# A three-part decoder layer on one core: feed-forward bias in row groups, reciprocal parts on another engine, input loads on another queue, and a new planned order

## The chip, the core and the metric

The kernel runs on one core of a Trainium2 chip. The core has a matrix engine (TensorE, PE in the profile, with its weight loads as PEld), three engines for elementwise work (VectorE or DVE, ScalarE or ACT, GpSimd or POOL) and SyncE (SP), which issues DMAs. All of them run at the same time, each through its own queue of instructions in order. The metric is the device time of one execution in microseconds (us).

## The reference

Eight sequences of 256 tokens with 512 features pass a self-attention with rotary positions, a cross-attention to a second input of the same shape, and a feed-forward part; behind each stands a layer norm of the sum with its input. The change touches what lies around the feed-forward part:

```python
def activation_quant(x):
    scale = 127.0 / jnp.clip(jnp.max(jnp.abs(x), axis=-1, keepdims=True), EPS, None)
    return jnp.clip(jnp.round(x * scale), -128.0, 127.0) / scale
def weight_quant(w):
    scale = 1.0 / jnp.clip(jnp.mean(jnp.abs(w)), EPS, None)
    return jnp.clip(jnp.round(w * scale), -1.0, 1.0) / scale
def bitlinear(x, w, b):
    return jnp.einsum('bsd,fd->bsf', activation_quant(x), weight_quant(w)) + b
h = bitlinear(x, w1, b1)                 # 512 -> 2048
h = jax.nn.gelu(h, approximate=False)
h = layernorm(h, gamma, beta)            # over 2048
return bitlinear(h, w2, b2)              # 2048 -> 512
```

## The kernel before, in words

The 2048 tokens are 16 tiles (tt) of 128. The residual lies in SBUF for the whole run as `acc`, 16 tiles of 128x512.

The first part, up to about 942 us, is the self-attention, with an order written out by hand (`SCHED`). The change does not touch it.

Everything after it is one planned stage. Each function (`kv`, `q`, `x`, `ffn_tables`, `ffn`) only records steps with `S(...)`: a step has one or more choices of engine with a cost in us, the tiles that it reads, writes and makes, and a function that issues its instructions. The planner at the end of `decoder_kernel` then plays the stage in its own clock: it takes the ready step with the lowest priority number that finds its engine and its buffers free, notes where it runs, and at last issues all steps in that order, engine by engine. Priorities come from `PLAN["base"]` (one number per unit of work), `PLAN["off"]` (small offsets per step) and the step's distance from its unit's end. `PLAN["lim"]` and `PLAN["cap"]` limit buffers, `PLAN["eng"]` fixes the engine of each step that has a choice, and `PLAN["T"]` says when a step of the other activation table may be taken; exponentials have table E and gelus table G. "DVE+" and "POOL" steps share a port in the planner's model, "POOL-" steps hold it shortly. So a changed cost or a changed PLAN moves instructions of the whole stage, not of one place.

The units of the stage:

- `kv(bp)`: keys and values of the cross-attention, four times 512 tokens, eight products of 12 matmuls each (kvp), written to DRAM.
- `q(b)`: the first layer norm and the transposes of two token tiles (tp), and for each second b the query product (qp).
- `x(b)`, per sequence: scores (sc, L880), exponentials (pt, L884), clamps with the mask (L888), sums (den, L911) and values (av, L895); the reciprocal of the sums spread by a small matmul (rp, L930) and multiplied into u (L933); then per token tile the split cT (L950 to L952), the output product (xo), two norms, and the quantised input of the feed-forward part. `stats` (L753, L754) or `astats` on ScalarE (L757 to L761) take mean and variance; `rstd` (L764, L765) and `scale1` (L967 to L969) on GpSimd make the reciprocal deviations; `absmax` (L985 to L987) the scale of the quantisation; L1004 and L1008 the rounding into xq; L1006 adds b2 to `acc`.
- `inverse` in `x` (L993 to L1001, GpSimd): the bias b1 is added by the matmul that also multiplies x with the weights. The matmul's sum is later scaled by a1s, so b1 has to come in divided by that scale. `inverse` puts the reciprocal of the scale, split in three bf16 parts, as columns 0, 32, 64 (three times the first part), 33, 65 (twice the second) and 66 of a block of 128 columns beside the 512 quantised values in xq, and zeros in the rest.
- The xq of 128x640 is transposed by a DMA into xT (L1010) and written to DRAM as xqs (L1011).
- `ffn_tables`: loads the quantised weights (fw0, fw1), gamma, beta, and b1 broadcast to 96 rows (b1r), split in bf16 parts in rows 0 to 31, 32 to 63 and 64 to 95 of b1s (L1034, L1036); csp and csum correct an offset of the second product.
- `ffn(tt)`, per token tile: load xqs as xx (`load`, issued at L714 by SyncE); two groups of ten matmuls (up): per 512 columns four with xx (L1070) and one of 96 rows for the bias (L1071); gelu with accumulated sum (L1075); mean (L1080), square (L1084) and `spread` (L1089 to L1091) for the norm over 2048; the norm itself for the half hi on VectorE (L1095, L1108) and for the half lo on ScalarE, VectorE and GpSimd (L1103, L1105, L1107); the maxima (L1111), `scale` (L1116 to L1118), L1121 on GpSimd; rounding into hq (L1124 ScalarE or L1125 VectorE); a DMA transpose into hT (L1153, for the last tile by TensorE, L1145); 17 matmuls (dn, L1131, L1133); y (L1155), its norm (L753, L754, L764, L765, L768, then L1160 VectorE or L1161 ScalarE) and the store of y (L1162).

Of the kernel before, what the change touches and what calls it, by code (L numbers as in the profile page):

```python
# [37 lines left out]
PLAN = {  # L38
    "base": {"c": [-3437], "wq": [-222], "wo": [2567], "kv": [774, 529, 640, 738], "q": [186, 220, 195, 464, 52, 506, 393, 405], "x": [-2946, -2928,
        -3094, -2933, -2926, -2955, -2930, -3031], "w": [2222], "f": [2732, 2741, 2722, 2769, 2648, 2719, 2728, 2753, 2749, 2721, 2720, 2716, 2739,  # L40
        2743, 2683, 2745]},
    "off": {"c": {0: 7, 1: -21, 3: 15, 4: 25, 5: 7, 7: -17, 8: -3, 9: 5}, "f": {0: -13, 1: 1, 2: -8, 3: 5, 5: -6, 6: 15, 9: -10, 10: -3, 11: 21, 12:
        16, 13: 5, 14: -20, 15: 12, 16: 20, 17: 7, 19: 7, 20: 2, 21: 3, 22: 30, 23: 5, 24: 3, 25: 27, 26: 5, 27: 11, 28: 10, 29: -8, 30: 2}, "kv": {1:
        3, 2: -9, 6: -23, 7: 10, 8: -3, 9: 5, 10: 3, 11: 9, 12: 3, 13: -22, 14: -6, 17: 11, 18: -3, 19: 24, 21: 17, 22: 3, 24: -11, 25: 5, 26: -6, 27:
        18, 28: -8, 29: -9}, "q": {0: 15, 5: 1, 6: -14, 7: 3, 8: 2, 9: 23, 12: 1, 13: -9, 14: -6, 15: -18, 16: 6, 17: -3, 18: 7, 19: -5, 21: -1}, "w":
        {0: -12, 1: -10, 2: 9, 3: 19, 5: 15, 6: 9, 7: 8, 9: -8, 12: -27, 14: -21, 16: -1, 17: -27, 18: 1, 19: -10}, "wo": {0: 6, 2: 4, 3: -27, 5: 1},
        "wq": {0: -16, 2: 6, 3: -21}, "x": {0: -3, 2: -16, 3: 10, 5: 13, 6: -2, 7: -18, 9: -8, 10: 6, 11: -9, 12: 4, 13: 12, 15: -3, 16: 10, 17: -3,
        19: -12, 20: -3, 23: -3, 24: 20, 25: 3, 26: -3, 28: -4, 29: -2, 30: -12, 31: -23, 32: -4, 33: 2, 34: 2, 36: 1, 38: 1, 39: -3, 41: -3, 42: 11,
        44: 6, 45: 8, 46: -4, 47: -1, 48: -7, 51: -1, 52: -13, 53: -17, 54: 18, 55: -4, 56: -20, 57: -5, 58: -1, 59: 8, 60: 14, 61: -14, 63: -7, 64:
        -8, 65: 10, 68: -5, 69: -11, 70: 10, 72: -11, 73: -3, 76: 3}},  # L50
    "lim": {"wqraw": 1, "kvp": 3, "kvs": 4, "cr": 1, "woraw": 1, "x1T": 1, "qst": 3, "tp": 1, "qp": 2, "kx": 2, "vx": 1, "u": 1, "rr": 2, "rs": 1,
        "den": 2, "pt": 4, "sc": 2, "av": 2, "rp": 2, "cT": 1, "d": 2, "xq": 2, "xT": 3, "xo": 2, "b1r": 1, "xx": 1, "h": 4, "hq": 3, "hT": 3, "y": 3,
        "up": 2, "dn": 1},
    "cap": {"p8": 6, "p4": 6, "p2": 9},
    "T": 1158, "hx": 1, "dve": [15], "sum": [],
    "eng": "0--1110100-0-010-0101-1-1-0--0-010-0-1-00-0-10-010-0101-1-1--010--1-00-11-000--0-010-010--0-1--1-0--0--0-1-0-00----010-0100---1--0"
        "00--00-0-1-100--010-0-011-0-1-000-000-000-00--00--010-001-0-0--00-0-0-00--000-01---",
}
# [20 lines left out]
def decoder_kernel(ctx: ExitStack, tc: tile.TileContext, a, out):  # L79
# [683 lines left out]
    def rstd(mv):  # L763
        nc.gpsimd.tensor_scalar(mv[:, 2:3], mv[:, 1:2], EPS, None, ALU.add)  # L764
        nc.gpsimd.tensor_tensor(mv[:, 3:4], mv[:, 2:3], nhalf, ALU.pow)  # L765
# [41 lines left out]
    def q(b):  # L807
# [5 lines left out]
        for t in range(2):  # L813
# [4 lines left out]
            S([("DVE", 0.8, lambda tt=tt, mq=mq: stats(acc[:, tt], H[mq]))], rd=[A], wr=[mq], new=[mq])  # L818
            S([("POOL-", 1.0, lambda mq=mq: rstd(H[mq]))], wr=[mq])
            S([("DVE", 0.13, lambda mq=mq: shift(H[mq]))], wr=[mq])  # L820
# [33 lines left out]
    def x(b):  # L854
# [80 lines left out]
        for qi in range(2):  # L935
# [29 lines left out]
            def scale1(m1=m1):  # L965
# [4 lines left out]

            S([("POOL-", 1.3, scale1)], wr=[m1])
            S([("DVE", 0.66, lambda ps=ps, m1=m1, d=d: nc.vector.scalar_tensor_tensor(H[d], H[ps], H[m1][:, 0:1], H["lng"], ALU.subtract, ALU.mult))],
# [4 lines left out]
               ("ACT", 2.1, lambda d=d, m2=m2, xq=xq: astats(H[d], H[m2], H[xq][:, 0:512]))], rd=[d], wr=[m2, f"{xq}/q"], new=[m2] + new(xq))  # L977
            S([("POOL-", 1.0, lambda m2=m2: rstd(H[m2]))], wr=[m2])
            S([("DVE", 0.13, lambda m2=m2: shift(H[m2]))], wr=[m2])
# [10 lines left out]

            def inverse(tt=tt, m2=m2, xq=xq):
                s, xq = H[m2], H[xq]
                nc.gpsimd.tensor_tensor(a1s[:, tt : tt + 1], s[:, 10:11], wscale[:, 0:1], ALU.mult)  # L993
                nc.gpsimd.memset(xq[:, 512:640], 0.0)
                inv = s[:, 12:13]
                nc.gpsimd.tensor_tensor(inv, s[:, 11:12], wscale[:, 2:3], ALU.mult)
                for n in (3, 2, 1):
                    c0 = 512 + 33 * (3 - n)
                    nc.gpsimd.tensor_copy(xq[:, c0 : c0 + 32 * n - 31 : 32], inv.to_broadcast([128, n]))
                    if n > 1:  # L1000
                        nc.gpsimd.tensor_tensor(inv, inv, xq[:, c0 : c0 + 1], ALU.subtract)  # L1001

            S([("POOL-", 2.0, inverse)], rd=[f"{m2}/s"], wr=[f"{xq}/i", f"a1s:{tt}"], new=new(xq))
            S([("ACT", 0.71, lambda tt=tt, d=d, m2=m2: nc.scalar.activation(H[d], acc[:, tt], AF.Identity, bias=magic, scale=H[m2][:, 11:12]))],  # L1004
# [9 lines left out]
    def ffn_tables():  # L1014
        unit[0] = ("w", 0)
        for wi in range(2):
            key = f"fw{wi}"
            mk(key, "xt", [128, 8192], (BF16, F16)[wi])
            for c in range(4):
                cs = slice(2048 * c, 2048 * c + 2048)  # L1020
                load(key, wq_s[wi][:, cs], 2.8, rd=["ks3:0"], part=f"/{c}", f=lambda t, cs=cs: t[:, cs])
        for n in ("g2", "be2"):
            mk(n, "w", [128, 2048])
            load(n, a[n].to_broadcast([128, 2048]), 5.0, rd=["ks2:3"])
        mk("b1s", "w p4", [96, 2048], BF16)
        for c in range(4):
            r, cs = f"b1r{c}", slice(512 * c, 512 * c + 512)
            mk(r, "p2", [96, 512])
            load(r, a["b1"][:, cs].to_broadcast([96, 512]), 1.1, rd=["ks2:3"])

            def rows(r=r, cs=cs):
                t, b1s = H[r], H["b1s"]
                for n in (96, 64, 32):
                    nc.vector.tensor_copy(b1s[0:n, cs], t[0:n])  # L1034
                    if n > 32:
                        nc.vector.tensor_tensor(t[0 : n - 32], t[0 : n - 32], b1s[0 : n - 32, cs], ALU.subtract)  # L1036

            S([("DVE+", 2.5, rows)], wr=[r, f"b1s/{c}"], new=new("b1s"))
        bank("csp")
        mk("cone", "p2", [128, 128], F16)  # L1040
        S([("POOL", 0.3, lambda: nc.gpsimd.memset(H["cone"], 1.0))], wr=["cone"], new=new("cone"))

        def sums():
            for k in range(16):
                nc.tensor.matmul(H["csp"], H["cone"], H["fw1"][:, 512 * k : 512 * k + 512], start=k == 0, stop=k == 15)

        S([("PE", 3.6, sums)], rd=["cone"] + [f"fw1/{c}" for c in range(4)], wr=["csp"], new=["csp"])
        S([("DVE", 0.6, lambda: nc.vector.tensor_copy(csum, H["csp"]))], rd=["csp"], wr=["csum"])

    def ffn(tt):  # L1050
# [8 lines left out]
        mk(my, "mv", [128, 16])  # L1059
        load(x2, xqs[tt], 0.9, rd=[f"xqs{tt}"])  # L1060
        for g in range(2):
# [3 lines left out]
            def up(g=g, ps=ps):  # L1065
                for c in range(2):
                    o = H[ps][:, 512 * c : 512 * c + 512]
                    f0 = 1024 * g + 512 * c
                    for k in range(4):
                        nc.tensor.matmul(o, H[x2][:, k], H["fw0"][:, 2048 * k + f0 : 2048 * k + f0 + 512], start=k == 0, stop=False)  # L1070
                    nc.tensor.matmul(o, H[x2][0:96, 4], H["b1s"][:, f0 : f0 + 512], start=False, stop=True)  # L1071

            S([("PE", 2.25, up)], rd=[x2] + [f"fw0/{c}" for c in range(4)] + [f"b1s/{c}" for c in range(4)], wr=[ps, f"{h}/{g}"],
              new=[ps] + new(h))
# [17 lines left out]

        S([("POOL-", 1.3, spread)], rd=[f"{st}/m"], wr=[f"{st}/q"])
        lo, hi = slice(0, HP), slice(HP, 2048)
# [19 lines left out]
        def scale():  # L1114
            s = H[st]
            nc.vector.tensor_tensor(s[:, 8:9], s[:, 8:9], s[:, 9:10], ALU.max)  # L1116
            nc.vector.tensor_scalar(s[:, 8:9], s[:, 8:9], EPS, 1.0 / 127.0, ALU.max, ALU.mult)
            nc.vector.reciprocal(s[:, 9:10], s[:, 8:9])  # L1118
# [38 lines left out]
        S([("DVE", 0.8, lambda: stats(H[y], H[my]))], rd=[y], wr=[my], new=[my])  # L1157
        S([("POOL-", 1.0, lambda: rstd(H[my]))], wr=[my])
        S([("DVE", 0.13, lambda: shift(H[my]))], wr=[my])
# [265 lines left out]
```

## Time and profile before

| what | value |
|---|---|
| runs | median 1388.79 us of 3 (1388.67 to 1389.3) |
| the profiled execution | 1388.65 us, span from first to last instruction 1386.9 us |
| mean granted TensorE clock | 0.99 |
| planned stage, first TensorE work | 942.5 us |
| last exponential ends | 1201.4 us |
| last store of y issued behind y15 | 1383.8 us |
| share of the chain that ended last | TensorE 81%, VectorE 11%, GpSimd 3%, ScalarE 2% |
| b1 parts on VectorE (L1034, L1036) | 1061.3 to 1097.7 us, 20 rows |
| xx, issue to landing | 2.3 / 2.6 / 4.4 us (least, median, most) |

How to read it: the span is one execution. A row of the profile gives engine, line, operation, what it writes from what it reads, shapes, how often, the busy time, the mean of one, and the idle time of the engine ahead of it with what ended that. In a timeline a row starts with the start and the duration in us; idle time ahead of it stands in brackets at its end with the releaser. Rows of one engine overlap by some hundredths, so a row's price is the distance from its start to the next one's start. SPq is SyncE's queue, and its rows are the time that issuing a DMA takes there, not the transfer.

### The profile page before, as it was taken

What the parts mean: (1) busy time and instruction counts of PE and PEld (TensorE: products, weight loads), DVE (VectorE), ACT (ScalarE), POOL (GpSimd) and SP (SyncE); (2) the same over time, 40 slices, a digit from 0 to 9 for tenths busy, and PEclk for the clock granted to TensorE, in tenths of its full rate; (3) what the DMA queues carried; (4) which work ended last, traced back from release to release, by engine and by line L of the source; (5) the groups of instructions that cost most, each with busy time, mean ns of one, the idle gap of its engine ahead of it and who ended that gap; (6) DMA issues with size and microseconds to landing.
All of it is one profiled execution on the core that took longest, in us unless ns stands there. A gap on an engine that the chain in (4) does not pass through costs nothing.

```text
span 1386.9 us, 23784 instructions
## 1 busy us (share of the span) xinstructions
PE 1346.3 (97%) x8576; PEld 1080.5 (78%) x8576; DVE 1092.0 (79%) x2040; ACT 879.7 (63%) x1948; POOL 782.6 (56%) x985
## 2 busy tenths in 40 slices
PE   9899999999999999999999999999999999987996
PEld 7789888998889888998899888887667767543442
DVE  6877767778768888887877876968667867798997
ACT  4666776766676666666665666634644445576994
POOL 5656556656665666766665656525033324386763
PEclk9999999999999999999999999999999999999998
DMA  8442342234222244223422342225324425214443
GB/s 316 175 186 108 124 170 107 92 118 172 110 76 96 92 155 164 104 84 135 180 85 99 130 172 107 69 99 190 115 62 123 145 64 161 72 34 97 111 110 99
DMA packets 85046, 170.13 MB, mean 123 GB/s; under 512 B 47040, under 2 KB 57024, under 8 KB 80064
## 3 DMA queue, kind: packets, MB, share of 16 engines
q1 hardware_dynamic: 84928, 168.61, 35.9%
q8 instruction: 68, 1.11, 0.3%
q14 instruction: 50, 0.41, 0.1%
HBM read 130.31 MB, written 27.79 MB: 114 GB/s over the span
## 4 chain that ended last, share of the span: by engine, by line
PE 81%; DVE 11%; POOL 3%; ACT 2%; issue 2%; DMA 1%; SPq 0%; POOLq 0%; DVEq 0%; ACTq 0%
PE ppj L146 12%; PE ppj L147 12%; PE ppj L148 12%; PE pz L146 3%; PE pz L148 3%; PE pz L147 3%; PE pwt L426 3%; PE sc L880 3%; PE den L911 2%; PE av L895 2%; PE ppo L146 2%; PE ppo L147 2%; PE ppo L148 2%; PE psc L376 2%; PE pz L449 2%
## 5 line engine op out<-in xcount | busy, mean ns | idle before, releaser
L324 POOL TENSOR_TENSOR sw<-sw,stab 128x512 f32<-128x512 f32 x128 | 170.8, 1334 | 101.3 <-ACT sw L315 100.7
L146 PE MATMUL ppj<-xt,w 128*128 128x512 f32 x528 | 209.0, 396 | 0.0
L147 PE MATMUL ppj<-xt,w 128*128 128x512 f32 x528 | 206.5, 391 | 1.0 <-DVE xt L157 0.4
L148 PE MATMUL ppj<-xt,w 128*128 128x512 f32 x528 | 206.3, 391 | 0.0
L146 PE MATMUL ppj<-w,xt 128*128 128x256 f32 (+1 forms) x528 | 157.3, 298 | 1.1 <-DVE u L320 1.1
L348 POOL TENSOR_TENSOR rh<-u,rh 128x512 fp32r<-128x512 f32 x64 | 97.4, 1522 | 100.1 <-PE ppj L148 91.5
L147 PE MATMUL ppj<-w,xt 128*128 128x256 f32 (+1 forms) x528 | 151.9, 288 | 0.0
L148 PE MATMUL ppj<-w,xt 128*128 128x256 f32 (+1 forms) x528 | 151.8, 288 | 0.0
L320 DVE SCALAR_TENSOR_TENSOR u<-ppj,bqk,ctab 128x512 f32<-128x512 f32 x128 | 95.6, 747 | 70.8 <-ACT sw L315 70.3
L314 ACT ACTIVATE sw<-ppj,bqk 64x512 f32<-64x512 f32 x128 | 87.7, 685 | 93.1 <-PE ppj L148 88.3
L332 POOL TENSOR_TENSOR u<-u,sw 128x256 f32<-128x256 f32 (+1 forms) x128 | 130.5, 1019 | 0.3 <-DVE u L320 0.2
L419 DVE SCALAR_TENSOR_TENSOR e<-aw,rd,sg 128x128 f32<-128x128 f32 (+1 forms) x256 | 125.9, 549 | 0.1
L148 PEld LDWEIGHTS ppj<-xt,w 128*128 128x128 f32 x528 | 99.1, 188 | 21.6 <-DVE w L183 0.4
L406 ACT ACTIVATE aw<-aw,nm 128x256 f32<-128x256 f32 (+1 forms) x256 | 113.3, 443 | 4.0 <-DVE nm L397 4.0
L391 POOL TENSOR_SCALAR_AFFINE_SELECT aw<-aw 128x256 f32<-128x256 f32 x128 | 59.7, 489 | 98.4 <-ACT aw L385 98.4
L453 ACT CAST z<-pz 128x512 fp32r<-128x512 f32 x64 | 37.6, 587 | 121.3 <-PE pz L449 121.3
L147 PEld LDWEIGHTS ppj<-xt,w 128*128 128x128 f32 x528 | 99.3, 188 | 18.0 <-DVE xt L183 0.8
L146 PEld LDWEIGHTS ppj<-xt,w 128*128 128x128 f32 x528 | 99.3, 188 | 16.7 <-ACT xt L285 0.4
L146 PEld LDWEIGHTS ppj<-w,xt 128*128 128x128 f32 x528 | 101.8, 193 | 2.0 <-DVE u L320 1.4
L147 PEld LDWEIGHTS ppj<-w,xt 128*128 128x128 f32 x528 | 102.0, 193 | 0.6
L148 PEld LDWEIGHTS ppj<-w,xt 128*128 128x128 f32 x528 | 101.8, 193 | 0.7
L385 ACT ACTIVATE aw<-psc 128x384 f32<-128x384 f32 x128 | 62.2, 486 | 60.5 <-PE psc L148 59.8
(283 smaller groups left out, 3937.4 us busy)
## 6 DMA issues: line engine op xcount, KB each, us to landing
xt<-xs SPq DMA_DIRECT2D x28, 2048.0 KB, 8.2
xs<-xt SPq DMA_DIRECT2D x4, 2048.0 KB, 12.8
raw<-w1T SPq DMA_DIRECT2D x16, 512.0 KB, 9.5
raw<-w2T SPq DMA_DIRECT2D x16, 512.0 KB, 9.4
acc<-xn SPq DMA_DIRECT2D x4, 1024.0 KB, 8.5
raw<-wO SPq DMA_DIRECT2D x8, 512.0 KB, 9.5
wq<-wqt SPq DMA_DIRECT2D x16, 256.0 KB, 2.4
kx<-ks SPq DMA_DIRECT2D x8, 512.0 KB, 5.3
```

What stands on the lines that cost most here:

```text
L146: nc.tensor.matmul(ps, lh, rh, start=first, stop=False)
L147: nc.tensor.matmul(ps, lh, rl, start=False, stop=False)
L148: nc.tensor.matmul(ps, ll, rh, start=False, stop=last)
L314: nc.scalar.activation(sw[0:64], ps[64:128], AF.Identity, bias=bias[64:128])
L320: nc.vector.scalar_tensor_tensor(v3(u), v3(self.ps.pop((h, i))), self.bias(h, i), ctab.to_broadcast([128, 2, 256]), ALU.add, ALU.mult)
L324: nc.gpsimd.tensor_tensor(v3(sw), v3(sw), stab.to_broadcast([128, 2, 256]), ALU.mult)
L332: nc.gpsimd.tensor_tensor(u, u, sw, ALU.add)
L348: (nc.gpsimd if i else nc.vector).tensor_tensor(lo, u if i else u[:, :, 128:256], f32(hi), ALU.subtract)
L385: nc.scalar.activation(aw[:, h], sc3, AF.Abs, scale=1.0 / math.sqrt(DH))
L391: nc.gpsimd.affine_select(aw[:, :, blk], aw[:, :, blk], pattern=[[0, 2], [-1, 128]], compare_op=ALU.is_ge, fill=MASKED, base=0, channel_mu ...
L406: nc.scalar.activation(aw[:, h, blk], aw[:, h, blk], AF.Exp, bias=nm[:, h, i : i + 1], accum_out=rd[:, h, i : i + 1])
L419: nc.vector.scalar_tensor_tensor(e[:, h, blk], aw[:, h, blk], rd[:, h, i : i + 1], sg[:, h, blk], ALU.mult, ALU.mult)
```

## The change

Five edits go together.

1. The bias columns: the six parts stand next to each other in columns 0 to 5 of each of four groups of 32 columns; b1 is loaded as 4 x 32 rows, one 512-column piece per group of 32 rows, split in three parts and combined by masks made of sums of columns of the identity into a b1s of 128x512. The bias matmul has six rows, and the two of a group of `up` stand behind its eight others, in two different groups of rows and with two different outputs.
2. `inverse` can run on GpSimd or ScalarE; zeros are written by a step of their own, earlier. In the new order 15 of the 16 tiles have ScalarE.
3. The load of xx is issued by ScalarE's queue instead of SyncE's. The planner still books it on SyncE.
4. In `scale` the maximum of the two halves and EPS is one tensor_scalar with a pointer operand instead of a tensor_tensor; in `rstd` the tensor_scalar has two operations instead of one.
5. Costs of GpSimd steps are raised in the planner, and PLAN has other numbers throughout: the order of the whole planned stage is new.

```diff
-    "T": 1158, "hx": 1, "dve": [15], "sum": [],
+    "T": 89, "hx": 2, "dve": [15], "sum": [],
...
     def rstd(mv):
-        nc.gpsimd.tensor_scalar(mv[:, 2:3], mv[:, 1:2], EPS, None, ALU.add)
+        nc.gpsimd.tensor_scalar(mv[:, 2:3], mv[:, 1:2], 1.0, EPS, ALU.mult, ALU.add)
...
+            S([("POOL-", 0.25, lambda xq=xq: nc.gpsimd.memset(H[xq][:, 512:640], 0.0))], wr=[f"{xq}/z"], new=new(xq))
...
-            def inverse(tt=tt, m2=m2, xq=xq):
-                s, xq = H[m2], H[xq]
-                nc.gpsimd.tensor_tensor(a1s[:, tt : tt + 1], s[:, 10:11], wscale[:, 0:1], ALU.mult)
-                nc.gpsimd.memset(xq[:, 512:640], 0.0)
+            def inverse(e, tt=tt, m2=m2, xq=xq):
+                s, xq4 = H[m2], H[xq][:, 512:640].rearrange("p (g r) -> p g r", g=4)
+                scalar = e is nc.scalar
                 inv = s[:, 12:13]
-                nc.gpsimd.tensor_tensor(inv, s[:, 11:12], wscale[:, 2:3], ALU.mult)
-                for n in (3, 2, 1):
-                    c0 = 512 + 33 * (3 - n)
-                    nc.gpsimd.tensor_copy(xq[:, c0 : c0 + 32 * n - 31 : 32], inv.to_broadcast([128, n]))
-                    if n > 1:
-                        nc.gpsimd.tensor_tensor(inv, inv, xq[:, c0 : c0 + 1], ALU.subtract)
+                if scalar:
+                    e.activation(inv, s[:, 11:12], AF.Identity, scale=wscale[:, 2:3])
...
+                for c0, n in ((0, 3), (3, 2), (5, 1)):
+                    part, src = xq4[:, :, c0 : c0 + n], inv.rearrange("p (g r) -> p g r", g=1).to_broadcast([128, 4, n])
+                    if scalar:
+                        e.copy(part, src)
+                        if n > 1:
+                            e.activation(inv, H[xq][:, 512 + c0 : 513 + c0], AF.Identity, scale=-1.0, bias=inv)
...
+                if scalar:
+                    e.activation(a1s[:, tt : tt + 1], s[:, 10:11], AF.Identity, scale=wscale[:, 0:1])
...
+            S([("POOL-", 3.4, lambda f=inverse: f(nc.gpsimd)), ("ACT", 1.5, lambda f=inverse: f(nc.scalar))],
...
-        mk("b1s", "w p4", [96, 2048], BF16)
+        mk("b1r", "p2", [128, 512])
         for c in range(4):
...
+            load("b1r", a["b1"][:, 512 * c : 512 * c + 512].to_broadcast([32, 512]), 0.5, rd=["ks2:3"], part=f"/{c}",
+                 f=lambda t, c=c: t[32 * c : 32 * c + 32])
...
+        def parts():
+            t, p, m = H["b1r"], H["b1p"], H["b1m"]
+            for i in range(3):
+                nc.vector.tensor_copy(p[:, i], t)
+                if i < 2:
+                    nc.vector.tensor_tensor(t, t, p[:, i], ALU.subtract)
...
+            nc.vector.tensor_scalar(H["b1s"], p[:, 0], m[:, 0:1], None, ALU.mult)
+            for i in (1, 2):
+                nc.vector.scalar_tensor_tensor(H["b1s"], p[:, i], m[:, i : i + 1], H["b1s"], ALU.mult, ALU.add)
...
-        load(x2, xqs[tt], 0.9, rd=[f"xqs{tt}"])
+        S([("SP", 0.9, lambda: nc.scalar.dma_start(H[x2], xqs[tt]))], rd=[f"xqs{tt}"], wr=[x2], new=[x2])
...
-                    nc.tensor.matmul(o, H[x2][0:96, 4], H["b1s"][:, f0 : f0 + 512], start=False, stop=True)
+                for c in range(2):
+                    r = 32 * (2 * g + c)
+                    nc.tensor.matmul(H[ps][:, 512 * c : 512 * c + 512], H[x2][r : r + 6, 4], H["b1s"][r : r + 6], start=False, stop=True)
...
-            nc.vector.tensor_tensor(s[:, 8:9], s[:, 8:9], s[:, 9:10], ALU.max)
-            nc.vector.tensor_scalar(s[:, 8:9], s[:, 8:9], EPS, 1.0 / 127.0, ALU.max, ALU.mult)
+            nc.vector.tensor_scalar(s[:, 8:9], s[:, 8:9], s[:, 9:10], EPS, ALU.max, ALU.max)
+            nc.vector.tensor_scalar(s[:, 8:9], s[:, 8:9], 1.0 / 127.0, None, ALU.mult)
```

In the order behind the last score matmuls, TensorE has before: den7, csp ahead of the last two score groups, then up00 between av71 and xo12, up01, rp7, xo13, up10, xo14, up11, xo15. After: csp behind the last scores, den7, av71, xo12, xo13, av7, rp7, up00, up01, xo14, xo15, up10, up11. From there on both alternate two groups of `up` with one `dn` some four tiles behind. Of the choices of engine behind that point, hq has 30 halves on ScalarE instead of 25, and the last norm of y has 10 tiles on ScalarE instead of 13.

## The prediction

> **What bounds the kernel now.** I read the page's busy lines and slices first, then a table of windows over the last stage, then the waits and the timelines of each engine there, then single rows.
>
> The page, engines and slices (a slice is 34.7 us):
>
> ```profile
> PE 1346.3 (97%) x8576; PEld 1080.5 (78%) x8576; DVE 1092.0 (79%) x2040; ACT 879.7 (63%) x1948; POOL 782.6 (56%) x985
> ...
> PE   9899999999999999999999999999999999987996
> ...
> DVE  6877767778768888887877876968667867798997
> ```
>
> TensorE is full until slice 35. Up to there only less TensorE work or a hole in it moves the end. The change begins in the planned stage (first TensorE work 942.5 us); before it both programs are the same on every engine. The windows behind the last exponential (ends 1201.4; its clamp on VectorE 1202.9):
>
> ```profile
> core 0: us, PE busy (x) PEld busy (x) DVE busy (x) ACT busy (x) POOL busy (x), PEclk, DMA share, GB/s
> 1203.00:1223.00 20.00, 20.00 (x127) 12.21 (x125) 15.35 (x28) 10.73 (x16) 8.60 (x17) 1.00 0.08 25
> 1223.00:1243.00 20.00, 14.14 (x57) 6.66 (x56) 18.58 (x39) 16.22 (x26) 17.43 (x33) 0.91 0.20 50
> 1243.00:1263.00 20.00, 12.09 (x50) 4.96 (x49) 16.01 (x28) 11.13 (x16) 14.42 (x25) 0.83 0.43 88
> 1263.00:1283.00 20.00, 18.28 (x85) 7.92 (x84) 18.42 (x29) 16.30 (x19) 11.95 (x15) 1.00 0.42 89
> 1283.00:1303.00 20.00, 16.97 (x79) 7.31 (x78) 19.31 (x34) 18.18 (x22) 15.42 (x17) 1.00 0.49 108
> 1303.00:1353.00 50.00, 48.61 (x225) 21.61 (x224) 49.31 (x88) 48.41 (x61) 34.26 (x45) 1.00 0.48 110
> ```
>
> From 1203 VectorE is the fullest engine: 137 of 150 us, TensorE 130. In the last row VectorE and ScalarE are both full; the L1095 rows there stand 8.16 us apart, which is the price of a feed-forward tile. So what can be won is the 13 us that VectorE lacks up to 1303, and what stands in them. Five rows from the timelines of SyncE, TensorE, GpSimd, VectorE and ScalarE show the largest hole:
>
> ```profile
> 1245.58 6.66 SPq L1010 DMA_TRANSPOSE xT<-xq  x2
> 1255.32 1.89 PE L1070 MATMUL up<-fw,xx 128*128 128x512 bf16 x4 [7.39 <-DMA xx<-xqs]
> 1250.96 4.64 POOL L1107 TENSOR_TENSOR h<-h,be 128x1024 f32<-128x1024 f32 x2
> 1253.33 2.35 DVE L1111 TENSOR_REDUCE fs<-h 128x1 f32<-128x1024 f32 x2 [3.07 <-POOL h L1107]
> 1256.23 1.24 ACT L1124 ACTIVATE hq<-h,half,fs 128x1024 f16<-128x1024 f32 x1 [7.06 <-POOL fs L1121]
> ```
>
> GpSimd made the reciprocal parts of tiles 14 and 15 from 1242.5 to 1251.0, so the two adds of L1107 came late, VectorE waited 3.07 us and ScalarE 7.06. The same parts held up the transposes on SyncE, behind which the load of xx5 stood: TensorE waited 7.39 us, then ran the next matmuls at half pace (four in 1.89 us, not 1.03).
>
> **The change, part by part.**
>
> *Bias matmul.* 64 matmuls of 96 rows become 64 of six rows, two and two in different row groups and different banks.
>
> ```profile
> 1202.82 1.03 PE L1070 MATMUL up<-fw,xx 128*128 128x512 bf16 x4
> 1203.68 0.38 PE L1071 MATMUL up<-b1s,xx 96*128 96x512 bf16 x1
> ...
> 1029.96 1.15 PE L880 MATMUL sc<-qst,kx 32*128 32x256 f32 x16
> ```
>
> Four stand 0.86 us from start to the next start, 0.215 each. A pair costs 0.215 (side by side) to 0.43 (one by one). The score rows use four row groups: 16 pieces of 256 columns in 1.08 us, 0.067 each, where 256 columns by the first row would be 0.108; by that ratio, 0.62, a pair takes 0.27. It saves 32 x 0.16 = 5 us of TensorE (0 to 7). None of it is on the path: TensorE has 20 us free from 1203 to 1353, and a steady tile of 8.16 us needs 37 x 0.215 = 7.96 of it. Worth 0. The Trainium skill ("TensorE: Matmul & The Clock Gate", Part 3) says that matmuls in different row groups run together and gives 3.07 times for four; by that a pair would be, as an estimate, 0.22 to 0.28, and the sum the same.
>
> *The bias rows on VectorE.* 12 copies (median 0.418) and 8 subtractions (0.682) go, 10.5 us; 3 copies, 2 subtractions, a scaled copy, two 512-wide adds (0.74 by L974) and nine tiny rows (0.15) come, about 6 us. Both lie before 1200, where TensorE is full and VectorE about 75% busy: 0.
>
> *Reciprocal parts.* 15 of 16 tiles go from GpSimd (9 rows, 2.4 us when nothing disturbs, 8.5 for two tiles above) to ScalarE: 7 rows that follow each other. The tiny ScalarE rows L758 to L761 stand 0.13 to 0.23 apart: about 1.45 us a tile. Six of these tiles (10 to 15) come behind the last exponential, 8.7 us, where ScalarE had 18 us free (1203 to 1263: 38.1 of 60 busy). For the earlier nine ScalarE is under 60% busy; but an exponential queued behind one comes up to 1.45 us later. Other matmuls cover that in the new order; without cover it would be a hole in TensorE.
>
> *xx loads from ScalarE.* 16 issues leave SyncE. They pass the transposes of xT and hT that they stood behind, and the stores of y; transposes and stores in turn come no later than before. On ScalarE an issue stands between two activations. It waits for xqs, written long before (except perhaps the last), and for a free slot; behind it are a gelu or the next square, and TensorE waits for those. ScalarE issues nothing now, so the price is bounded from below by 0 (the issue goes on beside the running activation of 1 to 2 us) and from above by SyncE's 16 xx rows: 0.32 to 1.29, median 0.69. I take 0.1, near to nothing, because ScalarE's rows follow one another without a gap, many of them behind a wait that was met early, so its queue is read ahead of the engine; 0.69 and more stay for the range. The skill ("Perfetto Trace Analysis", DMA Instruction — HWDGE) speaks against the change: the block that makes descriptors is locked for one issuer at a time, so an issue from ScalarE could wait out a transpose of SyncE. No row of before can show that; by the rule the sum would be that of the slow rival below, by rows alone it is the forecast.
>
> *L1116 and the tiny GpSimd rows.* The maximum of two numbers becomes a tensor_scalar.
>
> ```profile
> L1116 DVE TENSOR_TENSOR fs<-fs x16: 125/152/2184, 1233.5 to 1370.5; 128x1 f32<-128x1 f32 x16
> ```
>
> Its median is 0.152; the 2.18 (at 1272.8, beside a GpSimd row) and a 0.79 are waits. The tensor_scalar rows of L1117 never leave 0.153 to 0.155. If that form does not wait, 2.7 us of VectorE's time go, both before 1275. L764 with two operations instead of one: 0.222 to 0.190 by L1089, nothing on the path.
>
> *The new order.* I counted rows in both orders and priced each by its start-to-start time. Ahead of the last score matmul TensorE has 251.1 us of work instead of 251.6: -0.5. On VectorE behind the last clamp: one more product with rp 0.61, casts and differences of cT +0.5, one absmax group 0.82, two b2b adds 1.22, two xq rows 0.70, csum 0.60, three y rows 1.50, small change -0.13, five hq rows fewer -3.30. That is 155.2 to 157.7, +2.5. The five hq rows go to ScalarE (5 x 1.13), three y rows leave it (3 x 0.70).
>
> Then the idle time. Before 1300 VectorE's single waits over 0.15 us are 2.81, 1.17, 0.30, 0.88, 0.20, 3.07, 0.46, 0.23, 0.86, 0.46, 0.24, 0.18 = 10.9. The first feed-forward rows come later on VectorE (first matmuls behind xo13 and rp7, about 1217 instead of 1202), but the norms of tiles 12 to 15 fill that time, and the csum and reciprocal rows stand where it waited 2.81. I walked the new order row by row up to the scale of tile 4: waits of about 2 us before the first gelu (u7 and rp7), then 1.3, 2.4, 2.1 and 0.4 for gelus and squares, since ScalarE is now the full engine from 1217 to 1260. Together 8.2, so -2.7. Rows stretched beside GpSimd (L1105 1.66 instead of 1.21) -0.5.
>
> *Steady tiles and tail.* VectorE's per-tile rows are the same. ScalarE's too, up to one hq half more and two y fewer in 11 tiles, plus the issue. The tail (TensorE waits 2.96 for hT14, then PE transposes, y15, store) has the same rows in the same order: 0.
>
> **Sum.** -0.5 + 2.5 - 2.7 - 2.7 - 0.5 = -3.9, and for the issues +0.4 (0.04 in each of 10.5 steady tiles, see the slow rival): -3.5. The profiled execution took 1388.65 (span 1386.9 and 1.75 around it; the median of the runs is 1388.79, 0.14 more). So 1385.15 by its own time and 1385.3 by the median: **1385**.
>
> **Rivals.**
> - *The holes close altogether.* ScalarE's waits in my walk hang on a few tenths each. If all 10.9 us go: -0.5 + 2.5 - 2.7 - 10.9 - 0.5 = -12.1, 1376.5. For it: GpSimd no longer holds anything at 1242 to 1256, TensorE has xx early. Against: ScalarE gets about 13 us more work behind the last exponential (132.8 to about 146 without the issues).
> - *It washes out.* VectorE idles as long as before: -0.5 + 2.5 - 2.7 - 0.5 = -1.2, 1387.5. The bias pairs may also not run together, which alone changes nothing (7.96 under 8.16).
> - *ScalarE's queue becomes the bound (slower).* The place is the issue between two gelus in the steady tiles. ScalarE needs 1.98 (square) + 2 x 1.09 (gelu) + 1.14 (L1103) + 2 x 1.13 (hq) + 9/11 x 0.70 (y) - 0.05 = 8.1 us of the 8.16 there, so an issue of d costs d - 0.06 in each of 10.5 tiles. At 0.43 the gain of 3.9 is gone; from 0.7 on the kernel is slower by over 0.2%. At 1.05 (seven of SyncE's ten xx rows from 1261 on took 0.95 to 1.29): +10.4 - 3.9 = +6.5, 1395. For it: both engines are at 97% or more, and nothing is shorter in a steady tile. Against: the issue would have to keep the engine itself, not only its queue, for the whole time.
> - *Holes in TensorE before 1199*, from exponentials behind the parts: nine tiles at 0.6 us, +5.4 - 3.9: 1390.
>
> **Chances.** Forecast (1380 to 1386) 0.32, holes close (below 1380) 0.26, wash (1386 to 1391.6) 0.16, ScalarE's queue 0.18, holes in TensorE 0.08; of the last, half falls within 0.2%. About 0.2% (2.8 us) is what a measurement of this kernel can tell from no change. Faster 0.58, same 0.20, slower 0.22. The range goes from 1374 (holes close and a little of the tail) to 1393 (issue at 0.85: +8.3 - 3.9); even with no wait at all but the tail the floor is 1202.4 + 155 + 9 + 1.75 = 1368.
>
> **What would show it.** Right: no TensorE wait for xx over 1 us behind 1220; no VectorE wait on L1107 near 1250; the new maximum rows all near 0.15; steady tiles still 8.1 to 8.2 apart; bias pairs 0.22 to 0.27; TensorE full to 1199. Wrong: steady tiles above 8.5 with ScalarE gaps at the xx issues; TensorE idle ahead of score or den matmuls before 1199; the first gelu later than 1219 with VectorE empty.

## The result, and the profile after

The changed kernel takes **1395.82 us** (median of 6 runs, 1394.83 to 1397.09), the kernel before, run beside it, 1388.73 (6 runs): ratio 1.0054, 95% interval 1.0043 to 1.0065. Run once more (e18 below) it gave 1.0055. The forecast was 1385, faster; the change made the kernel 7 us slower, and the time lies above the range of 1374 to 1393. The profiled execution took 1397.09 with a span of 1395.3, 8.4 more than the span before.

The page of the changed kernel, engine slices (34.9 us each):

```profile
PE   9899999999999999999999999999999999979877
...
DVE  6877777778768887888787877959687676888997
```

Nothing shows up to slice 35. Behind it the slices shift: TensorE has 8 and 7 tenths in slices 38 and 39, before 9 and 9, but 9 instead of 7 in slice 37. The stretches that the prediction showed, now of the changed kernel:

```profile
core 0: us, PE busy (x) PEld busy (x) DVE busy (x) ACT busy (x) POOL busy (x), PEclk, DMA share, GB/s
...
1223.00:1243.00 20.00, 15.20 (x67) 7.30 (x66) 18.37 (x40) 18.91 (x40) 14.10 (x20) 0.96 0.31 57
1243.00:1263.00 20.00, 12.36 (x47) 4.29 (x46) 15.20 (x28) 18.09 (x28) 9.84 (x13) 0.87 0.47 95
...
1303.00:1353.00 50.00, 46.26 (x202) 18.61 (x202) 46.16 (x73) 41.96 (x51) 32.47 (x37) 0.93 0.41 94
```

The stretch where the prediction looked for its gain (1223 to 1263) is as full as it was on VectorE (33.6 us busy, before 34.6), while ScalarE has 9.7 us more there. The steady one, 1303 to 1353, is not: there VectorE was 49.31 us busy of 50, now 46.16, and ScalarE fell from 48.41 to 41.96. A large part of the loss stands where the prediction had put a zero.

To see it in numbers I took the last clamp on VectorE as a mark and went down VectorE's timeline from there. Each kind of row has a price, the lower quartile of its distances from start to next start over all runs of this study; what a distance exceeds its price by is "held"; bracketed time is "idle". The walk goes through one execution of each kernel, for the changed kernel the slowest of its six; single executions of one kernel differ by up to 6 us (e1's went from 1390.22 to 1396.33), so differences of 1 or 2 us between such sums say little by themselves. In us:

| | last clamp ends | to the last VectorE row | rows | idle | held |
|---|---|---|---|---|---|
| before | 1203.0 | 180.8 | 155.9 | 16.5 | 7.8 |
| after | 1205.2 | 187.0 | 158.3 | 17.1 | 11.1 |
| before, first 80 us | | 80 | 63.6 | 10.4 | 6.0 |
| after, first 80 us | | 80 | 68.2 | 8.0 | 3.9 |

(Rows, idle and held leave 0.5 us at the end over.) So 2.2 us are lost ahead of the clamp and 6.2 behind it. Eighty us behind the clamp the changed kernel is ahead: 4.6 us more of its rows are done, of a sum that is 2.4 longer. From there on it idles 3.0 longer (9.1 against 6.1) and its rows are held 5.4 longer (7.2 against 1.8), while 2.2 fewer remain: +6.2.

**Ahead of the clamp.** TensorE was full before; now it has a hole. Timelines of VectorE, GpSimd and TensorE after (start, duration):

```profile
950.67 3.02 DVE L820 TENSOR_SCALAR acc<-acc,mq 128x512 f32<-128x512 f32 x2
...
951.04 2.37 POOL L737 TENSOR_TENSOR wq<-wqraw,wq 128x1024 fp32r<-128x1024 f32 x1
...
953.75 0.66 PE L825 MATMUL tp<-ident,acc 128*128 128x128 f32 x4 [2.73 <-DVE acc L820]
...
956.06 0.63 PE L146 MATMUL kvp<-xt,w 128*128 128x512 f32 x1
```

Two normalisations that take 1.0 us together took 3.02, beside a GpSimd row on two inputs. TensorE stood 2.73 us for the second, and for some 3 us its next matmuls ran at half pace (0.43 from start to start instead of 0.23). A second hole, 1.14 at 1045.98, has the same shape: two clamps beside the low part of ctx.

```profile
1042.41 3.52 DVE L886 TENSOR_SCALAR pt<-pt,mkf 128x1024 f32<-128x1024 f32 x2
...
1042.57 2.80 POOL L785 TENSOR_TENSOR ctx<-cr,ctx 128x1024 fp32r<-128x1024 f32 x1 [4.44 <-DVE ctx L783]
...
1045.98 1.07 PE L893 MATMUL av<-pt,vx 128*32 128x256 f32 x16 [1.14 <-DVE pt L886]
```

**Behind the clamp** the two largest held rows, VectorE's and GpSimd's timelines after:

```profile
1287.07 2.35 POOL L1131 TENSOR_TENSOR h<-h,be 128x1024 f32<-128x1024 f32 x1
1287.22 2.49 DVE L1184 TENSOR_SCALAR y<-y,my 128x512 f32<-128x512 f32 x1
...
1339.32 4.58 DVE L1132 SCALAR_TENSOR_TENSOR h<-h,fs,be 128x1024 f32<-128x1024 f32 x2
1339.48 3.33 POOL L1131 TENSOR_TENSOR h<-h,be 128x1024 f32<-128x1024 f32 x1
```

A norm of y that takes 0.55 alone took 2.49, and a pair worth 2.4 took 4.58: 4.1 us in two places, both beside the adds of be on GpSimd. TensorE's waits in the same stage, after:

```profile
PE dn L1155 <- DMA hT<-hq: 18.8, 5, 4.8
PE up L1092 <- DMA xx<-xqs: 4.8, 2, 3.6
```

And before:

```profile
PE up L1070 <- DMA xx<-xqs: 16.1, 7, 7.4
PE dn L1131 <- DMA hT<-hq: 4.9, 3, 3.0
```

TensorE waits less for xx and more for hT. Most of that comes with the order: e1 below, which issues xx from SyncE again, has 14.5 for hT and 5.8 for xx. What VectorE waits for dn fell behind 1285 (2.7 us, 4.2 before), which speaks against this trade as the place of the loss. The chain of work that ended last speaks for it. In the changed kernel it passes a transpose of hT four times behind the clamp, 19.6 us in all, two of them between tiles:

```profile
1298.89 4.82 DMA hT<-hq
...
1353.01 4.71 DMA hT<-hq
```

In the kernel before it passes none behind the clamp. The changed kernel run once more (e18) has the same four. No run edits these transposes, so late hT stays an untested rival for what is lost behind the clamp.

One place stands out. The means of the 13th and the 14th tile on VectorE (L1104) are 13.9 us apart in the changed kernel and were 7.9 apart before. TensorE runs two dn one behind the other there (1330.56 to 1338.07) before the up of the later tile. Every run of the new order below has 13.8 or 13.9 in this place, e1 too, and every run of the old order 7.9 or 8.0: it is the order's, and no edit inside a step moved it.

### The profile page after: what moved, and what is told of

It is laid out like the page before. It is cut to its first block, busy times and chain, and to the rows that moved or that the text cites. A ratio compares the mean times of both kernels' runs of the same rounds, so it can differ in the third digit from the quotient of the medians.

```text
span 1395.3 us, 23799 instructions
## 1 busy us (share of the span) xinstructions
PE 1349.5 (97%) x8576; PEld 1078.2 (77%) x8576; DVE 1096.5 (79%) x2046; ACT 902.0 (65%) x2053; POOL 752.8 (54%) x876
## 3 DMA queue, kind: packets, MB, share of 16 engines
q1 hardware_dynamic: 82368, 165.46, 34.9%
```

## The experiments

Each was timed in five rounds beside the kernel before. "The new order" is the changed kernel's, "the old order" the one before; an edit inside a step leaves the order as it is.

| run | kernel | median us | ratio, interval |
|---|---|---|---|
| e1 | new order, old instructions | 1393.82 | 1.0034 (1.0023 to 1.0046) |
| e2 | old order, new instructions | 1399.30 | 1.0076 (1.0063 to 1.0089) |
| e5 | old order, instruction forms alone | 1385.76 | 0.9985 (0.9977 to 0.9994) |
| e6 | old order, xx from ScalarE alone | 1387.02 | 0.9989 (0.9980 to 0.9998) |
| e7 | old order, first 13 parts on ScalarE | 1399.10 | 1.0076 (1.0062 to 1.0089) |
| e8 | old order, last 3 parts on ScalarE | 1389.57 | 1.0008 (0.9999 to 1.0017) |
| e9 | old order, forms and xx | 1385.69 | 0.9982 (0.9973 to 0.9991) |
| e3 | new, first norm on ScalarE | 1391.89 | 1.0021 (1.0013 to 1.0030) |
| e14 | new, low part of wq on VectorE | 1394.41 | 1.0037 (1.0025 to 1.0050) |
| e13 | e3, and low part of ctx on VectorE | 1391.04 | 1.0016 (1.0008 to 1.0025) |
| e4 | new, all norms of y on ScalarE | 1395.15 | 1.0048 (1.0036 to 1.0060) |
| e17 | e13, five hq halves on VectorE | 1390.79 | 1.0015 (1.0006 to 1.0024) |
| e10 | new, parts on GpSimd | 1396.86 | 1.0060 (1.0047 to 1.0073) |
| e11 | new, xx from SyncE | 1392.76 | 1.0041 (1.0028 to 1.0053) |
| e12 | new, 96-row bias | 1392.82 | 1.0041 (1.0027 to 1.0055) |
| e16 | new, old forms | 1393.30 | 1.0037 (1.0024 to 1.0049) |
| e15 | new, e3 with e11 and e12 | 1391.34 | 1.0019 (1.0010 to 1.0028) |
| e18 | the changed kernel again | 1396.84 | 1.0055 (1.0042 to 1.0068) |

**Order or instructions: e1 and e2.** My first theory was that the order costs the 7 us and the instructions nothing.

```diff
 e1, in the changed kernel: nc.scalar.dma_start(H[x2], ...) -> nc.sync; both choices of inverse on nc.gpsimd;
     the maximum as tensor_tensor; rstd's first row with one operation (the bias in row groups stays)
 e2, in the old kernel: the reverse of these four (the old layout of the columns and the 96-row bias stay)
```

> The new order with the old instructions: parts on GpSimd for every tile, xx issued by SyncE, the maximum as a tensor_tensor, the one-operation row in rstd. Bias in row groups and the new order stay. Theory A (the order costs the 7 us, the instructions are worth nothing or a little): 1394 to 1400, that is the changed kernel's 1395.8 or somewhat above it, since the waits at the maximum and the parts on GpSimd come back. Theory B (the order is harmless, ScalarE's extra work and its issues cost the 7 us): 1386 to 1390.

> The old order with the new instructions: all parts on ScalarE, xx issued by ScalarE, the maximum as a tensor_scalar, the two-operation row in rstd; bias matmul as before. Theory A (order): 1382 to 1388, since L1116's 3 us of waits and GpSimd's hold near 1250 go. Theory B (instructions): 1393 to 1398.

Both theories fail. The order, with the bias in row groups, costs 4.8 us (0.34%), but the instructions alone, in the old order, cost 10.6: each half of the change is slower by itself, and together they are not the sum. e2's last clamp came at 1213.1, ten us late.

**Which instruction: e5 to e8,** one edit each in the old kernel.

```diff
 e5: -nc.vector.tensor_tensor(s[:, 8:9], s[:, 8:9], s[:, 9:10], ALU.max)
     +nc.vector.tensor_scalar(s[:, 8:9], s[:, 8:9], s[:, 9:10], EPS, ALU.max, ALU.max)   (and rstd)
 e6: -load(x2, xqs[tt], ...)   +S([("SP", 0.9, lambda: nc.scalar.dma_start(H[x2], xqs[tt]))], ...)
 e7: inverse on nc.scalar (memset stays on GpSimd) for the first 13 tiles issued
 e8: the same for the last 3 alone
```

> The old kernel with the two instruction forms alone: the maximum as a tensor_scalar, two operations in rstd's first row. If the waits at the maximum vanish with the form, as the prediction had it: 2 to 3 less, 1386 to 1387. If the wait only moves to the next VectorE row that a GpSimd row can hold: 1389, no change.

> The old kernel with the xx loads alone issued by ScalarE. An issue takes 0.33 us of ScalarE's queue beside a running row, so by itself nothing; the loads no longer stand behind the transposes on SyncE but behind whatever ScalarE has ahead of them. Theory A (the 10 us of the old order with new instructions are the parts' alone): 1387 to 1391. Theory B (the late issues are a large share): 1393 to 1398.

> The old kernel with the reciprocal parts of the first 13 tiles on ScalarE, the last three on GpSimd. Theory A (exponentials queued behind 1.8 us of tiny rows open holes in TensorE up to the last score matmuls, and the half clock behind a hole doubles them): last clamp 8 to 10 us later, 1396 to 1400. Theory B (these tiles are covered): 1388 to 1390.

> The old kernel with the reciprocal parts of the last three tiles on ScalarE, where no exponential is left. If GpSimd's hold near 1250 was worth what the prediction gave it: 1385 to 1388. If ScalarE's 5.4 us more in the start-up of the feed-forward part weigh as much: 1389 to 1392.

e5: the maximum no longer waits, as forecast. In e5's timelines it stands beside the same GpSimd row that held it for 2.18 us before:

```profile
1272.23 3.34 POOL L1107 TENSOR_TENSOR h<-h,be 128x1024 f32<-128x1024 f32 x1 [1.70 <-DVE h L1105]
...
1273.39 0.21 DVE L1116 TENSOR_SCALAR fs<-fs 128x1 f32<-128x1 f32 x1
```

VectorE's way from the last clamp to its end fell from 180.8 to 178.0, about the 2.7 of the prediction; but only 1.2 of it is held time, 1.8 is idle time, and the rows cost 0.2 more. e6 gains 1.5; the issue takes 0.33 us of the queue while ScalarE's rows go on, so the price of 0.1 was near. e7 is the whole loss of e2. Timelines of ScalarE and TensorE in e7:

```profile
1058.24 0.53 PE L146 MATMUL kvp<-w,ctx 128*128 128x512 f32 x1 [1.89 <-DVE kvs L802]
...
1203.41 1.00 ACT L884 ACTIVATE pt<-sc 128x1024 f32<-128x1024 f32 x1
1204.67 0.30 ACT L1007 ACTIVATE mb<-mb,wscale 128x1 f32<-128x1 f32 x1 [0.25 <-DVE mb L987]
...
1206.45 1.00 ACT L884 ACTIVATE pt<-sc 128x1024 f32<-128x1024 f32 x1
...
1207.51 1.13 PE L880 MATMUL sc<-qst,kx 32*128 32x256 f32 x12 [1.30 <-ACT pt L884]
```

The seven tiny rows stand between the two exponentials of one score group and take 1.78 us from the first to the exponential (the estimate was 1.45). Four holes ahead of score matmuls, 2.8 us together, end with an exponential. The largest, 1.89, does not: it ends with a VectorE row (L802), and the eight matmuls behind it run at half pace. Ahead of L802 stands a cast that takes 0.69 in the kernel before. VectorE and GpSimd in e7:

```profile
1055.83 1.75 DVE L785 CAST ctx<-cr 128x1024 fp32r<-128x1024 f32 x1
...
1055.53 1.50 POOL L1022 TENSOR_TENSOR acc<-acc,b2b 128x512 f32<-128x512 f32 x1 [1.03 <-ACT d L1020]
```

The parts made ScalarE's d later, GpSimd's add waited for it, and it fell beside the cast. The holes sum to 5.8 us (0.8 before), the last clamp is 9.4 late. This is, for about half of the holes, the prediction's rival of holes in TensorE, in the order for which it did not stand; the largest hole is again a VectorE row beside a GpSimd row. In the new order the only hole ahead of the clamp that ends with ScalarE is one of 0.15 us.

e8 gains nothing. VectorE idles less (13.1 against 16.5), but the GpSimd rows, free of the parts, meet other VectorE rows, held 12.3 instead of 7.8:

```profile
1250.65 5.21 POOL L1123 TENSOR_TENSOR h<-h,be 128x1024 f32<-128x1024 f32 x2 [3.58 <-DVE h L1121]
...
1250.82 2.84 DVE L1022 TENSOR_TENSOR acc<-acc,b2b 128x512 f32<-128x512 f32 x1
...
1253.66 3.28 DVE L1124 SCALAR_TENSOR_TENSOR h<-h,fs,be 128x1024 f32<-128x1024 f32 x1
```

**The holes ahead of the clamp: e3, e14, e13.**

```diff
 e3, in q, the DVE+ choice:  +nc.scalar.activation(acc[:, tt], ..., AF.Identity, bias=..., scale=...) if tt == 0 else ...
 e14, in weight, low part:   -nc.gpsimd   +nc.vector if n == "wq" else nc.gpsimd
 e13, e3 and in kv, low part: -nc.gpsimd   +nc.vector if bp == 3 else nc.gpsimd
```

> The changed kernel with one row moved: the first normalisation of token tile 0 (L820, held 2.4 us beside the low part of wq on GpSimd) runs on ScalarE in the same place of the order. If the hole of 2.73 us in TensorE at 951 and the half clock behind it are paid to the end, as the 2.2 us by which the last clamp is later say: 1392 to 1394 (2 to 4 less). If the late part of the kernel has slack for it: 1395.8, no change.

> The changed kernel with the other side of the first meeting taken away: the low part of wq (L737, 2.37 us on GpSimd at 951) runs on VectorE behind the two normalisations, which stay there. If GpSimd's row is what held L820: L820's two rows take about 1 us instead of 3.02, the hole in TensorE shrinks to 1.3 or less, 1391 to 1393. If the hole comes from the place of L820 in VectorE's order: 1395 to 1397.

> The changed kernel with the first normalisation on ScalarE, as in e3, and the low part of ctx at 1042 (L785, 2.80 us on GpSimd, beside which two clamps took 3.52 instead of 1.35 and TensorE stood 1.14) on VectorE. If a GpSimd row on two inputs holds VectorE's tensor_scalar rows and this is the second hole's cause: 1 to 2 less than e3, 1390 to 1391. If that hole has slack behind it: 1391.9, as e3.

e3 gives 3.9 us back, more than the 2.2 by which the clamp was late: with the shorter hole (1.26) the clock stays at 1.00 from 955 to 965, where the changed kernel had 0.85. e14 takes away the other partner, and the normalisations stay where they were:

```profile
949.61 1.00 DVE L820 TENSOR_SCALAR acc<-acc,mq 128x512 f32<-128x512 f32 x2
...
950.66 0.66 PE L825 MATMUL tp<-ident,acc 128*128 128x128 f32 x4 [0.76 <-DVE acc L820]
...
965.67 0.63 PE L825 MATMUL tp<-ident,acc 128*128 128x128 f32 x4 [1.47 <-DVE x1T L829]
```

1.00 instead of 3.02: the GpSimd row was what held them. The low part now costs VectorE 1.2, and another hole opens at 965; the clamp is 2.5 earlier. The time at the end moved by 1.4 (2.4 against e18), less than e3's 3.9 and than expected, and its interval touches that of the changed kernel. e13 closes the second hole, with 1.20 left of the first, and its last clamp comes at 1201.0, 2.0 earlier than before; its ratio, 1.0016, lies inside e3's interval, so the second hole's price isn't resolved.

The Trainium skill ("SBUF — State Buffer", SBUF: two separate sides) says that VectorE and GpSimd share a pair of ports by an exclusive lock, taken for a whole instruction, by GpSimd or by a VectorE row in a two-port mode or with two inputs in SBUF. The rows here agree: a 512-wide tensor_scalar (L820, L1184) and rows on two tiles (L1132, and L1022 in e8) are held, a one-column tensor_scalar isn't (0.18 to 0.21 in all 16 rows).

**Is VectorE the bound behind the clamp: e4 and e17.**

```diff
 e4:  -nc.vector.tensor_scalar(H[y], H[y], ..., ALU.mult, ALU.add)   +nc.scalar.activation(H[y], H[y], AF.Identity, ...)
 e17: hq of (0, 1), (1, 0), (1, 1), (2, 1), (8, 1): nc.scalar.activation -> nc.vector.tensor_scalar
```

> The changed kernel with the six norm rows of y that stand on VectorE moved to ScalarE, in the same places of the order. If VectorE's rows count one to one behind the last clamp (six rows of 0.5, one of them held 2.0 longer beside GpSimd): 5 less, 1391. If ScalarE is as full as VectorE there (six rows of 0.7 more): 1395 to 1400.

> The kernel of e13 with five halves of the rounding into hq (tiles 0, 1, 1, 2 and 8, as in the old kernel) on VectorE instead of ScalarE, in the same places of the order. If ScalarE's fullness from 1240 to 1270 (a gelu waits behind four hq halves, VectorE and TensorE wait for it) is what the new order lost behind the last clamp: 2 to 4 less than e13, 1387 to 1389. If VectorE's rows count one to one: 3.3 more, 1394. If neither is full alone and the chain goes from one to the other: 1390 to 1392.

| from the last clamp | length | rows | idle | held |
|---|---|---|---|---|
| after | 187.0 | 158.3 | 17.1 | 11.1 |
| e4 | 185.1 | 155.5 | 20.1 | 8.9 |
| e13 | 184.6 | 158.3 | 15.1 | 10.7 |
| e17 | 184.7 | 161.6 | 11.0 | 11.6 |

e4 took 5.0 us of rows and held time from VectorE, and 3.0 came back as idle time; by the median it gained 0.7. e17 gave it 3.3 us more, and idle time fell by 4.1. So in the new order rows moved to or from VectorE are mostly swallowed: it isn't the bound by itself. In the old order it was nearly that: from 100 to 160 us behind the clamp it doesn't idle at all, and the new order adds 3.3 us there.

**The other edits in the new order: e10, e11, e12, e16, e15, e18, e9.**

```diff
 e10: both choices of inverse on nc.gpsimd     e11: xx by nc.sync.dma_start     e16: the old forms of scale and rstd
 e12: one matmul of 96 rows behind each four, H[x2][0:96, 4] with H["b1s"][0:96]
 e15: e3, e11 and e12 together                 e18: no edit                     e9: e5 and e6 together
 (in e12 and e15 all pieces get the same 96 rows, so what is added isn't b1)
```

> The changed kernel with the reciprocal parts of all tiles back on GpSimd, in the same places of the order. If the parts on ScalarE cost in the new order what they cost in the old one (10.7): 1385 to 1388. If the new order covers those ahead of the last exponential (its holes in TensorE end with VectorE rows, none with ScalarE) and only the six tiles behind it count: between no change and 5 less, 1391 to 1396.

> The changed kernel with the xx loads issued by SyncE again. By the old order, where the move to ScalarE gained 1.5: 1396 to 1398. If the later issues of ScalarE are what makes tiles 12 to 15 late in the new order: 1388 to 1392.

> The changed kernel with one 96-row bias matmul behind each four, in the place it had before, instead of two six-row ones in different row groups; all 512-wide pieces get the same 96 rows of b1s, so what is added isn't b1. By the prediction's zero (TensorE isn't the bound): 1395 to 1397. If the pairs gain on the path, 5 us of TensorE in all: up to 1400.

> The changed kernel with the maximum as a tensor_tensor and the one-operation row in rstd. If the form is worth the 2.7 here that it was worth in the old order: 1398 to 1399. If the new order has no GpSimd row beside the maxima, or the wait only moves to the rows behind: 1395 to 1397.

> The changed kernel with three undone together: the first normalisation on ScalarE (e3, -3.9), xx from SyncE (e11, ratio 1.0041 instead of 1.0054, -2), 96-row bias matmuls (e12, 1.0041, -2; what is added isn't b1). If these add, the new order is worth nothing either way: 1387 to 1389. If xx and bias were only scatter: 1391 to 1393.

> The changed kernel itself once more, beside e17 on one chip, as a measure of scatter: its ratio was 1.0054, those of six kernels that undo one small thing each 1.0037 to 1.0060. If these differences are real: 1.0050 or more. If a repeat scatters by as much: between 1.0035 and 1.0050.

> The old order with the two edits that paid alone: the instruction forms (ratio 0.9985, that is -2.1) and the xx loads from ScalarE (0.9989, -1.5). If they add: 1384.5 to 1385.5. If both close the same wait: 1385.8 to 1387.

e10: moving the parts back gains nothing in the new order. e11, e12 and e16 each came out 1.8 to 2.4 us below the changed kernel by the ratio, which I did not expect; e18 says that the changed kernel's median is no accident. But the intervals touch, single executions of each go up to 1395.97, 1396.54 and 1397.35, and e15, which undoes two of them with the first hole closed, is where e3 alone is (1.0019, 1.0021). These gains do not add up, so they are no prices of xx, bias or forms. What they have in common I can't show.

The bias pairs, seen in the changed kernel's TensorE timeline:

```profile
1279.94 1.89 PE L1092 MATMUL up<-fw,xx 128*128 128x512 bf16 x8
1281.76 0.39 PE L1095 MATMUL up<-b1s,xx 6*128 6x512 bf16 x2
1282.08 1.90 PE L1092 MATMUL up<-fw,xx 128*128 128x512 bf16 x8
```

Ten matmuls from start to start take 2.14 us; with 96 rows in e12 (1280.18 to 1282.35) 2.17. The pair starts 1.82 behind the eight, 0.10 more than 8 x 0.215, and takes 0.32, again 0.10 more than one matmul. So the two seem to run side by side, and what that saves goes into two gaps of 0.10 around them. The skill ("TensorEngine Tiling (Array Packing)", Tiling Modes) says that changing the tiling mode drains TensorE, which would make such gaps; no run here separates it.

e9: forms and xx together give 0.9982, hardly more than the forms alone (0.9985). The sum of both gains, 0.9974, lies in its interval too, so whether they add or close the same waits isn't resolved. It has the lowest ratio here and is faster than the kernels before and after, but its lead over e5 isn't resolved.

## Why the prediction was wrong, step by step

- *TensorE ahead of the last score, -0.5.* The clamp came 2.2 later, not 0.5 earlier, for two holes where VectorE rows were held by a GpSimd row. With the first hole cut to 1.20 and the second closed (e13) it came 2.0 earlier, so the count of work had the right sign. I counted TensorE's rows and never walked VectorE's new order ahead of 1200 against GpSimd's; "TensorE is full and VectorE about 75% busy: 0" was the slip. My rival for this place named exponentials; in the old order (e7) the clamp came 9.4 late against the 5.4 given, but exponentials end only 2.8 of the 5.8 us of holes.
- *VectorE's rows behind the clamp, +2.5.* Measured 2.4.
- *L1116, -2.7, and stretched rows, -0.5.* In the old order the form is worth about 2.7 (e5), though less than half of that as held time, so the size is partly luck. In the new one the old form costs nothing that shows (e16, 1393.30); no maximum is held there, but other rows are: held time is 3.3 more, not 3.2 less. I priced a meeting of two engines as a property of one row; it is one of the order.
- *Idle time in the start-up, -2.7.* Up to 80 us behind the clamp it is 2.4 less. Right as far as I walked.
- *Steady tiles and tail, 0.* This is **the step that failed** by the largest sum: I stopped the walk at the scale of tile 4 and took the rest as unchanged, since the rows per tile are. From there on idle time is 3.0 more and held time 5.4 more. The first means of the last ten tiles stand 10.1 us apart on average (1277.5 to 1368.6; before 9.1, 1276.3 to 1358.5), where I gave 8.1 to 8.2 as a sign for steady tiles; 6.0 of the 8.9 us between the two sums stand in the one place shown above.
- *xx from ScalarE, +0.4.* Cheap, as taken: 0.33 beside a running row, and faster in the old order (e6). Three of the 16 issues began while SyncE was issuing a transpose of hT (at 1253.73, 1300.36 and 1328.71) and took 0.33 or 0.34 like the others, so none waited such an issue out, which was the case against. The slow rival that I gave 0.18, ScalarE's queue as the bound, is not what happened (ScalarE was 41.96 us busy of 50 from 1303 on), so that its 1395 is near the result is coincidence.
- *Parts on ScalarE, bias pairs.* 1.78 instead of 1.45 a tile, and taking them back gained nothing in the new order (e10). ScalarE had 21.9 us free from 1203 to 1263 by the rows shown, not 18. A pair costs 0.42, not 0.22 to 0.27; by e12 that cost the end nothing that is resolved.

In the sum's own terms: ahead of the clamp +2.2 (-0.5 forecast), rows +2.4 (+2.5), held +3.3 (-3.2), idle +0.6 (-2.7): 8.5 of the 8.4 that the span grew. Of the 7 us of the medians e3 gives 3.9 back by one moved row; e1 shows that the order, with the bias in row groups, costs 4.8. Which dependence sets the idle time of tiles 8 to 15 stays open: ScalarE, VectorE and the transposes of hT release each other in turn, and no single edit closed it. The 2 us that e13 and e17 are still slower than the kernel before are not explained either.

## What to carry to other kernels

When a planner writes a new order, walk it to the end on the pair of engines that hold each other, not only through the stretch that you mean to gain in: here the stretch walked came out nearly as forecast, and the 8.4 us were lost ahead of it and behind it. A form of instruction that was not seen held is worth taking in an order that stays as it is (e5, e9), and each edit of a bundle is worth timing alone in the old order first. A tiny row moved to another engine costs the distance to the next row of the critical chain there, 1.78 us between two exponentials.

## What the runs showed of the hardware that I had not expected

- 512-wide VectorE tensor_scalars beside a GpSimd row on two inputs ended behind it: 1.0 became 3.02 (L820, and 1.00 again when the GpSimd row was gone, e14), 0.55 became 2.49 (L1184). A one-column tensor_scalar beside such a row took 0.21 (e5).
- A hole of 2.73 us in TensorE cost more than itself: the granted clock was 0.85 from 955 to 965, and closing half of the hole gave 3.9 us at the end. After a hole of 1.26 (e3) it stayed at 1.00; behind one of 1.89 (e7) eight matmuls ran at half pace.
- Two six-row matmuls in different row groups behind full-height ones take 0.42 us, as long as two full ones (0.43).
